# A four-layer graph network kernel on Trainium2: the last propagation as seven half-size products, with the sums of adj stored part by part

## The chip, the cores and the metric

The kernel runs on one core of one Trainium2 chip. The metric is device time in microseconds (us): how long the core takes for one execution, from its first instruction to the last result in DRAM. A core has five engines with instruction streams of their own: TensorE (PE; its weight loads are shown apart as PEld), VectorE (DVE), ScalarE (ACT), GpSimd (POOL) and SyncE (SP). In this kernel nearly all large loads and stores are issued by SP, one after the other. All data is float32.

## The reference, cut to what matters

The input x has 3327 nodes with 256 features; adj is a sparse, symmetric-pattern 3327 x 3327 matrix kept dense. Four layers follow one another, each as x = x + layer(relu(layernorm(x))). The first three multiply adj (with some change) by a 3327 x 256 matrix each. The change concerns layer 3, and the writes that layers 0 and 2 make for it:

```python
R = S + eye(N);  R = R / R.sum(-1)          # S is adj
Z = 0;  Xf = X;  Xa = X
for n in range(2):                          # the two steps
    A = top_p_attention(Xa)                 # softmax rows, only the entries that make up 0.9
    Xf = R @ Xf                             # propagation
    Xa = A @ Xa                             # attention
    Z = Z + Xf @ U1[n].T + Xa @ U2[n].T
return layernorm(X + Z) * ln_g + ln_b
```

## The kernel before

**Tiles and pairs.** The nodes are padded to T = 26 row tiles of 128 (P); D = 256 is the number of features, H = 13 half the number of tiles. Tiles p and p + 13 form a pair. `adj_t[m, :, k, :]` in DRAM is the block of adj that gives row tile m its share from column tile k. Matrix products keep a 128 x 128 block of adj as the weights and stream the right side through PE. The profile shows each float32 matmul of the program as two records.

**Half-size products.** In layers 0 to 2, a pair's product of a 2 x 2 matrix of blocks (rows p and p + 13, columns in two halves) with a right side cut likewise (two halves of rows, two halves of 128 features) is made of 7 products instead of 8, as in Winograd's form of Strassen's method. For that, sums of adj are needed (four for each pair: s1, s2, s4 and one that is written over a21, made on DVE in `Feed.add`, L489 to L492) and sums of the right side. A pair's columns are taken in three parts (`CUTS`) of five, four and four tiles; (p, c) is part c of pair p. `Feed` loads a part's four blocks of adj ahead (L473, SP), adds them, and, for the pairs in `keep`, also stores the four sums in `s_dram` (L495, SP). Layer 3 reads them from there. Layer 0 stores pairs 2, 4 to 12, layer 2 stores pair 0 and the odd ones (`KEPT`, L613), each with all three parts. In layer 2 DVE also counts the positive entries of each loaded block. The rows of a finished pair go through stages (`Pair`, L350 to L443); there PE turns h3a, the normalized rows (L373), which DVE makes at L400.

**Layer 3, step 1** (985 to 1745 us of the trace, with its last two phases between 1745 and 1876) already takes the propagation as 7 products for each pair: `FirstStepsPair` (L1095) loads a slab of 13 blocks (832 KB, SP) from `adj_t` or `s_dram` for each product n, POOL adds the identity to one block of the slab for n = 1, 4, 5 and 7 (L1110, for R = S + I), and PE issues 13 matmuls with 128 columns (L1140). A pair has two phases, products 1, 2, 5, 4 and then 7, 3, 6 (`PHASES`), each with an accumulator of one PSUM bank. After the first phase `half` (ACT, L1149) copies that bank, after the second `whole` (DVE, L1159 to L1163) adds the parts to the two rows. The slabs lie in a pool with three buffers, so that a load waits until PE has used up the third slab before it. `combine_h3` makes the right sides' sums `ts`, once.

**Layer 3, step 2** (1876 to 2606 us) takes the tiles one by one, m = 0 to 25. For each, PE does two things. `rows.finish(m)` is the attention: it turns the row of weights e in blocks (L181), ACT copies them (L184), PE multiplies them with `vs` (L192). Then `propagate_second` issues 26 matmuls with 256 columns (L1078) over two slabs (L1075), POOL having added the identity to one block (L1077). Between those matmuls other work is put at given points: the logits of the tile three ahead (`AHEAD` = 3; `prepare`, two groups of PE work at L923, exponentials on ACT at L944), and at point 20 the first turns of the next tile's attention (`rows.begin`). PE executes in the order in which the program is written (`manual_schedule`); the other engines' order is planned by the framework, which puts `high_priority` work ahead.

DVE searches the threshold of each row of weights (`search_steps`, L948): one pass over e at L993, four at L1002 with 26 MAX8 instructions between them (L1006), a chain of short ones, and the pass at L1022 which sets e to what is kept. PE turns e after that. The passes of ACT for the same search (L977, L982) are placed with `passes` and `passes_apart`.

`finish3` (L1225 to L1247) ends a tile: SP loads z (L1229) and x3 (L1231), POOL adds y, the attention's result (L1232), DVE adds the propagated rows (L1234) and takes mean and variance (L1236, L1238), POOL takes the root (L93, L95), DVE scales (L1241), POOL does three additions and multiplications (L1243 to L1245; DVE for the last tile), and SP writes the rows to `out` (L1247).

Of the kernel before, what the change touches and what calls it, by code (L numbers as in the profile page):

```python
# [11 lines left out]
F32 = mybir.dt.float32  # L12
# [10 lines left out]
D = 256  # L23
# [22 lines left out]
def kernel(  # L46
# [221 lines left out]
    def layers_0_to_2(again):  # L268
# [186 lines left out]
        class Feed:  # L455
# [24 lines left out]
            def add(self, p, c):  # L480
                a, b = CUTS[c]
                name = f"{tag}{self.layer}_{p}_{c}"
                q = self.quads.pop((p, c))
                s1, s2, s4 = (
                    raw.tile([P, 5, P], F32, tag=f"s{n}", name=f"s{n}_{name}", bufs=2)[:, : b - a, :]
                    for n in (1, 2, 4)
                )
                a11, a12, a22, a21 = (q[ij] for ij in QUADS)
                nc.vector.tensor_tensor(s1, a21, a22, ALU.add)  # L489
                nc.vector.tensor_tensor(a21, a11, a21, ALU.subtract)  # L490
                nc.vector.tensor_tensor(s2, s1, a11, ALU.subtract)
                nc.vector.tensor_tensor(s4, a12, s2, ALU.subtract)  # L492
                if p in self.keep:
                    for n, s in enumerate((s1, s2, a21, s4)):
                        nc.sync.dma_start(s_dram[:, p, n, a:b, :], s)  # L495
                self.ready[p, c] = a11, a12, s4, a22, s1, s2, a21
# [116 lines left out]
        KEPT = range(2, H, 2), [0, *range(1, H, 2)]  # L613
        IN_ORDER = [(p, c) for p in range(H) for c in range(len(CUTS))]

# [234 lines left out]
    def layer_3_in(tag, big, ep, w3, sm3, h3, kT0, ksum0, left, at_end):  # L850
# [3 lines left out]
        ts = new_nodes(f"ts3{tag}").rearrange("p t d -> p (t d)")[:, : 4 * H * P]  # L854
        ts = ts.rearrange("p (n k f) -> p n k f", n=4, k=H)
# [229 lines left out]
        def combine_h3(a, b):  # L1085
            def part(i, j):
                return h3[:, i * H + a : i * H + b, j * P : (j + 1) * P]

            t1, t2, t3, t4 = (ts[:, n, a:b, :] for n in range(4))
            nc.vector.tensor_tensor(t1, part(0, 1), part(0, 0), ALU.subtract)  # L1090
            nc.vector.tensor_tensor(t2, part(1, 1), t1, ALU.subtract)
            nc.vector.tensor_tensor(t4, part(1, 0), t2, ALU.subtract)
            nc.vector.tensor_tensor(t3, part(1, 1), part(0, 1), ALU.subtract)

        class FirstStepsPair:  # L1095


            def __init__(self, p):
                self.p, self.accs, self.slabs, self.name = p, {}, {}, f"{tag}_{p}"

            def load(self, n):
                p = self.p
                x = self.slabs[n] = slabs.tile([P, H, P], F32, tag="slab", name=f"slab3{tag}_0_{p}_{n}")
# [8 lines left out]
            def right(self, n, k):  # L1112
                if n in (1, 2, 3):
                    i, j = {1: (0, 0), 2: (1, 0), 3: (1, 1)}[n]
                    return h3[:, i * H + k, j * P : (j + 1) * P]
                return ts[:, {5: 0, 6: 1, 7: 2, 4: 3}[n], k, :]

            def steps(self, phase):
# [11 lines left out]
                for at, (n, k) in enumerate(units):  # L1130
                    bank, c = PLACE3[n]
                    start = bank not in self.accs
                    if start:
                        self.accs[bank] = new_acc(f"f0_{self.name}_{bank}")
# [90 lines left out]
        def finish3(m, y, acc, name):  # L1225
# [4 lines left out]
            x3 = w3.tile([P, 4, P], F32, tag="xf", name=f"x3_{name}").rearrange("p n f -> p (n f)")[:, :D]  # L1230
            nc.sync.dma_start(x3, x3_dram[:, m, :])  # L1231
            nc.gpsimd.tensor_tensor(z, z, y, ALU.add)  # L1232
            with tc.high_priority():
                nc.vector.scalar_tensor_tensor(z, acc[:, :D], rinv[:, m : m + 1], z, ALU.mult, ALU.add)  # L1234
# [140 lines left out]

        with tc.manual_schedule(engines=PE_ALONE):
# [40 lines left out]
            def propagate_first(n, at):  # L1417

                p, phase = divmod(n, 2)
                pair = pairs.setdefault(p, FirstStepsPair(p))  # L1420
# [40 lines left out]
            with tc.issue_after(left.made.ins):  # L1461
                combine_h3(0, H - 1)
            combine_h3(H - 1, H)
# [75 lines left out]
            steps_of_second = prepare(1, 1, kT1)  # L1539
            spare.append(made[1][0])  # L1540
            pairs[H - 1] = FirstStepsPair(H - 1)
# [17 lines left out]

        only_exp_and_ln()  # L1560
        with tc.manual_schedule(engines=PE_ALONE):
# [6 lines left out]
            second = find(1, 1, st1)  # L1568
# [6 lines left out]
            propagate_first(T - 1, merged(spread(prepare(1, 2, kT1), 4, 10), plan))  # L1575
            run(second)
            finder = find(1, 2, st1)
# [14 lines left out]
            for m in range(T):  # L1592
                plan, later = passes_apart(1, finder) if m + AHEAD < T else (passes(finder), {})
                if m == 0:
                    p, q = props
                    plan = merged(plan, {2: [p.scale, q.scale], 4: [p.turn], 5: [p.sums, q.turn], 6: [q.sums]})
                acc = rows.finish(m, plan)
                if m == 0:
                    nc.sync.dma_start(gs, ln_g.partition_broadcast(P))
                    nc.sync.dma_start(bs, ln_b.partition_broadcast(P))  # L1600
                y = attention_of_second_step(m, acc, dens.pop(m), f"{m}")
                plan = spread(prepare(1, m + AHEAD, kT1)) if m + AHEAD < T else {}
                plan = merged(plan, {20: [lambda: rows.begin(m + 1)]}, later)
# [84 lines left out]
```

## Time and profile before

| | |
|---|---|
| median of 3 runs (lowest, highest) | 2623.57 us (2622.97, 2629.18) |
| time of the profiled execution | 2624.72 us |
| its span in the trace | 2622.9 us, 45628 instructions |
| mean granted clock of PE | 0.994 |
| PE, DVE, ACT, POOL busy | 97%, 78%, 41%, 13% |
| layers 0 to 2 | 0 to 985 us |
| layer 3, step 1 | 985 to 1876 us |
| layer 3, step 2, and the end | 1876 to 2623 us |

The profile comes from one execution. Its span is what the trace covers; its time is the device time of that same execution, and both stand beside the median of the runs that were only timed. The busy time of an engine is the sum of its instructions; those that run side by side on different engines are counted on each. A line like `L1078` is the line of the kernel from which an instruction comes. "Idle before" and the name after `<-` tell what ended an engine's wait, as far as semaphores show it. A granted clock of 1.00 is the full speed of PE.

### The profile page before, as it was taken

How to read it: one execution, taken by the hardware profiler on the slowest of the kernel's cores; microseconds unless marked ns; L12 is line 12 of the kernel's file. 1: busy time of each engine (PE TensorE's matmuls, PEld its weight loads, DVE VectorE, ACT ScalarE, POOL GpSimd, SP SyncE). 2: the span in 40 equal slices, each digit the busy share in tenths (PEclk: the TensorE clock that was granted, in tenths of full speed). 3: DMA queues.
4: the chain of work that ended last, by engine and by line, in shares of the span. 5: the costliest groups of instructions: out<-in, count | busy, mean ns of one | idle time of the engine just before them, and what ended most of it. 6: DMA issues, size and time to landing. Idle time of an engine off the chain costs nothing. (4 is left out here: it accounts for less than half of the span.)

```text
span 2622.9 us, 45628 instructions
## 1 busy us (share of the span) xinstructions
PE 2539.9 (97%) x16993; PEld 2238.4 (85%) x16993; DVE 2058.3 (78%) x5464; ACT 1076.4 (41%) x2042; POOL 330.5 (13%) x461
## 2 busy tenths in 40 slices
PE   6999999999999999999999999998999999999997
PEld 6999999999999997878787878887878887888786
DVE  6666688888777778787878788884888888888883
ACT  2110123343111115555656556544555555555541
POOL 2000010000000001000000000000122232223321
PEclk9999999999999999999999999999999999999998
DMA  6677665555778856323232323232521222122111
GB/s 211 193 244 230 210 212 165 178 173 166 255 257 267 274 186 207 105 65 106 72 109 77 105 66 105 83 117 76 169 71 65 75 81 71 65 81 77 68 66 52
DMA packets 176477, 357.66 MB, mean 136 GB/s; under 512 B 19043, under 2 KB 78048, under 8 KB 176224
## 3 DMA queue, kind: packets, MB, share of 16 engines
q1 hardware_dynamic: 147904, 333.64, 39.3%
q10 hardware_dynamic: 28320, 20.80, 2.5%
q8 instruction: 140, 2.29, 0.4%
q14 instruction: 113, 0.93, 0.1%
HBM read 284.77 MB, written 67.89 MB: 134 GB/s over the span
## 5 line engine op out<-in xcount | busy, mean ns | idle before, releaser
L184 ACT COPY eT_a<-pt_a 128x512 f32<-128x512 f32 (+1 forms) x364 | 195.8, 554 | 394.5 <-PE pt_a L181 394.3
L192 PE MATMUL a<-h3a,eT_a 128*128 128x256 f32 x1352 | 323.5, 381 | 0.2 <-ACT eT_a L184 0.2
L192 PE MATMUL a<-vs,eT_a 128*128 128x256 f32 x1352 | 320.2, 381 | 0.2 <-ACT eT_a L184 0.2
L1078 PE MATMUL f<-fsa,slab3a 128*128 128x256 f32 x1352 | 312.7, 382 | 0.0
L1078 PEld LDWEIGHTS f<-fsa,slab3a 128*128 128x128 f32 x1352 | 249.8, 189 | 52.7 <-issue 17.4
L1006 DVE MAX8 cand_a<-w 128x8 f32<-128x128 f32 x1352 | 288.6, 278 | 4.5
L192 PEld LDWEIGHTS a<-h3a,eT_a 128*128 128x128 f32 x1352 | 244.2, 189 | 36.9 <-issue 5.9
L192 PEld LDWEIGHTS a<-vs,eT_a 128*128 128x128 f32 x1352 | 246.3, 190 | 31.5 <-ACT eT_a L184 0.7
L527 PE MATMUL acc_a<-tsa,s_a 128*128 128x128 f32 (+1 forms) x2028 | 268.5, 275 | 1.7 <-DVE tsa L335 1.7
L527 PE MATMUL acc_a<-tsa,a_a 128*128 128x128 f32 x2028 | 252.0, 276 | 2.0 <-DVE tsa L338 2.0
L527 PE MATMUL acc_a<-rhs,a_a 128*128 128x128 f32 (+1 forms) x2028 | 250.7, 276 | 0.1
L527 PEld LDWEIGHTS acc_a<-tsa,s_a 128*128 128x128 f32 x2028 | 247.4, 192 | 2.4 <-DVE tsa L335 2.2
L527 PEld LDWEIGHTS acc_a<-tsa,a_a 128*128 128x128 f32 x2028 | 240.6, 193 | 3.6 <-DVE tsa L338 2.6
L527 PEld LDWEIGHTS acc_a<-rhs,a_a 128*128 128x128 f32 x2028 | 238.4, 192 | 2.2 <-ACT rhs L416 0.4
L1002 DVE SCALAR_TENSOR_TENSOR w<-e_a,t_a 128x896 f32<-128x896 f32 x208 | 225.1, 1082 | 4.3
L944 ACT ACTIVATE e_a<-pl_a 128x1024 f32<-128x1024 f32 x208 | 177.8, 859 | 122.8 <-PE pl_a L923 122.8
L181 PE MATMUL pt_a<-ident,e_a 128*128 128x128 f32 x1352 | 198.9, 273 | 6.6 <-DVE e_a L1022 6.4
L181 PEld LDWEIGHTS pt_a<-ident,e_a 128*128 128x128 f32 x1352 | 165.6, 141 | 38.6 <-DVE e_a L1022 7.0
L993 DVE SCALAR_TENSOR_TENSOR w<-e_a,t_a 128x3328 uint8<-128x3328 f32 x52 | 191.6, 3684 | 4.0 <-DVE t_a L990 0.9
L1022 DVE SCALAR_TENSOR_TENSOR e_a<-e_a,all_least 128x3328 f32<-128x3328 f32 x52 | 191.6, 3685 | 1.8
L376 ACT ACTIVATE xT_a<-pt_a 128x512 f32<-128x512 f32 x52 | 30.8, 593 | 361.3 <-PE pt_a L373 340.5
L1140 PEld LDWEIGHTS f_a<-ts3a,slab3a 128*128 128x128 f32 x1352 | 161.5, 192 | 20.3 <-issue 18.5
(225 smaller groups left out, 3864.1 us busy)
## 6 DMA issues: line engine op xcount, KB each, us to landing
a_a<-in_adj_t_dram SPq DMA_DIRECT2D x312, 256.0 KB, 3.9
slab3a<-in_adj_t_dram SPq DMA_DIRECT2D x91, 832.0 KB, 4.7
a_a<-in_adj_t_dram SPq DMA_DIRECT2D x156, 320.0 KB, 3.5
slab3a<-s_dram SPq DMA_DIRECT2D x52, 832.0 KB, 4.5
s_dram<-s_a SPq DMA_DIRECT2D x78, 256.0 KB, 3.1
s_dram<-s_a SPq DMA_DIRECT2D x39, 320.0 KB, 3.5
x_dram<-x_a ACTq DMA_DIRECT2D x39, 256.0 KB, 4.0
s_dram<-a_a SPq DMA_DIRECT2D x26, 256.0 KB, 4.7
```

Of the source, the lines that this page charges most:

```text
L181: nc.tensor.transpose(pt[:, j, :], e[:, k * P : (k + 1) * P], ident)
L184: last_turned.append(nc.scalar.copy(eT[:, : len(blocks), :], pt[:, : len(blocks), :]))
L192: nc.tensor.matmul(acc[:, :width], ready[g][:, j, :], rhs[:, k, :], start=(k == 0), stop=(k == T - 1))
L376: nc.scalar.activation(dst.rearrange("p f n -> p (f n)"), pt.rearrange("p f n -> p (f n)"), func)
L527: nc.tensor.matmul(self.acc[:, g, at : at + wide], quads[n][:, k - CUTS[c][0], :], t, start=(k == 0 and n in (1, 4)), stop=(k == H - 1 and ...
L944: last_exp.append(nc.scalar.activation(dst, src, AF.Exp, accum_out=parts[:, c : c + 1]))
L993: nc.vector.scalar_tensor_tensor(junk, e, t, e, ALU.is_lt, ALU.mult, accum_out=got)
L1002: nc.vector.scalar_tensor_tensor(w[:, : (b - a) * P], eg, t, eg, ALU.is_lt, ALU.mult, accum_out=below[:, g : g + 1])
L1006: nc.vector.max(cand[:, 8 * k : 8 * k + 8], w[:, (k - a) * P : (k - a + 1) * P])
L1022: nc.vector.scalar_tensor_tensor(e, e, least, e, ALU.is_ge, ALU.mult, accum_out=st["kept"][:, m : m + 1])
L1078: nc.tensor.matmul(acc[:, :D], slab[g][:, j, :], xf[:, k, :], start=(n == 0), stop=(n == T - 1))
L1140: nc.tensor.matmul(self.accs[bank][:, c * P : (c + 1) * P], a, self.right(n, k), start=start, stop=last.get(bank) == (n, k), skip_group_ch ...
```

## The change

1. *Step 2 of layer 3.* The pairs p = 1 to 12 are propagated as 7 half-size products, by the class of step 1, now with arguments and called `PropagatedPair`; tiles 0 and 13 stay as they were. The tiles of step 2 are taken in the order 0, 13, 1, 14, 2, 15 and so on (`ORDER`). The attention of tile p is followed by the first phase of its pair, that of tile p + 13 by the second phase, and then `finish3` runs for both. The points of the other work are scaled to the phase's number of matmuls (52 or 39 instead of 26).
2. *Sums of the right side.* `combine` makes them for step 2's right side `fs` in tile 13's attention, in three cuts, in a buffer of its own (`new_ts`).
3. *Sums of adj.* What is stored in `s_dram` is chosen by part instead of by pair: of the 39 parts (p, c), counted in order, layer 2 stores those of pairs 0 and 1 and the odd ones (22), layer 0 the even ones from pair 2 on (17).
4. *Buffers.* x3 takes a buffer of tag hT instead of xf, since `half` uses xf now. One column of `w` is set to 0 between the two sections.

```diff
@@ -490,7 +490,7 @@
                 nc.vector.tensor_tensor(a21, a11, a21, ALU.subtract)
                 nc.vector.tensor_tensor(s2, s1, a11, ALU.subtract)
                 nc.vector.tensor_tensor(s4, a12, s2, ALU.subtract)
-                if p in self.keep:
+                if (p, c) in self.keep:
                     for n, s in enumerate((s1, s2, a21, s4)):
                         nc.sync.dma_start(s_dram[:, p, n, a:b, :], s)
                 self.ready[p, c] = a11, a12, s4, a22, s1, s2, a21
...
@@ -610,8 +610,10 @@
         def from_rows(dram_rows):
             return lambda p, x2: nc.sync.dma_start(x2, pair_of(dram_rows, p))
-        KEPT = range(2, H, 2), [0, *range(1, H, 2)]
         IN_ORDER = [(p, c) for p in range(H) for c in range(len(CUTS))]
+        KEPT = [], []
+        for n, (p, c) in enumerate(IN_ORDER):
+            KEPT[p < 2 or n % 2].append((p, c))
         def counter(i):
...
@@ -851,8 +853,11 @@
-        ts = new_nodes(f"ts3{tag}").rearrange("p t d -> p (t d)")[:, : 4 * H * P]
-        ts = ts.rearrange("p (n k f) -> p n k f", n=4, k=H)
+        def new_ts(step):
+            t = new_nodes(f"ts{tag}_{step}").rearrange("p t d -> p (t d)")[:, : 4 * H * P]
+            return t.rearrange("p (n k f) -> p n k f", n=4, k=H)
+
+        ts = new_ts(0)
         vs = big.tile([P, T, D], F32, name="vs")
...
@@ -1082,9 +1087,9 @@
         FIRST_PHASES = (1, 2, 3), (5, 4, 7, 6)
         PLACE3 = {2: (0, 0), 1: (0, 1), 4: (0, 2), 5: (0, 3), 6: (1, 0), 7: (1, 1), 3: (1, 2)}
-        def combine_h3(a, b):
+        def combine(h, ts, a, b):
             def part(i, j):
-                return h3[:, i * H + a : i * H + b, j * P : (j + 1) * P]
+                return h[:, i * H + a : i * H + b, j * P : (j + 1) * P]
             t1, t2, t3, t4 = (ts[:, n, a:b, :] for n in range(4))
             nc.vector.tensor_tensor(t1, part(0, 1), part(0, 0), ALU.subtract)
...
@@ -1092,15 +1097,16 @@
             nc.vector.tensor_tensor(t4, part(1, 0), t2, ALU.subtract)
             nc.vector.tensor_tensor(t3, part(1, 1), part(0, 1), ALU.subtract)
-        class FirstStepsPair:
-
-
-            def __init__(self, p):
-                self.p, self.accs, self.slabs, self.name = p, {}, {}, f"{tag}_{p}"
+        class PropagatedPair:
+
+
+            def __init__(self, step, p, h, ts):
+                self.step, self.p, self.h, self.ts = step, p, h, ts
+                self.accs, self.slabs, self.name = {}, {}, f"{step}{tag}_{p}"
             def load(self, n):
                 p = self.p
-                x = self.slabs[n] = slabs.tile([P, H, P], F32, tag="slab", name=f"slab3{tag}_0_{p}_{n}")
+                x = self.slabs[n] = slabs.tile([P, H, P], F32, tag="slab", name=f"slab3{tag}_{self.step}_{p}_{n}")
                 if n in (1, 2, 4):
                     i, j = {1: (0, 0), 2: (0, 1), 4: (1, 1)}[n]
                     nc.sync.dma_start(x, adj_t[p + i * H, :, j * H : (j + 1) * H, :])
...
@@ -1112,8 +1118,8 @@
             def right(self, n, k):
                 if n in (1, 2, 3):
                     i, j = {1: (0, 0), 2: (1, 0), 3: (1, 1)}[n]
-                    return h3[:, i * H + k, j * P : (j + 1) * P]
-                return ts[:, {5: 0, 6: 1, 7: 2, 4: 3}[n], k, :]
+                    return self.h[:, i * H + k, j * P : (j + 1) * P]
+                return self.ts[:, {5: 0, 6: 1, 7: 2, 4: 3}[n], k, :]
             def steps(self, phase):
...
@@ -1222,16 +1228,16 @@
                 if not last:
                     nc.sync.dma_start(fs_dram[:, self.m, :], rows)
-        def finish3(m, y, acc, name):
+        def finish3(m, y, rows, name):
             z = w3.tile([P, D], F32, tag="z", name=f"z1_{name}")
             nc.sync.dma_start(z, z_dram[:, m, :])
-            x3 = w3.tile([P, 4, P], F32, tag="xf", name=f"x3_{name}").rearrange("p n f -> p (n f)")[:, :D]
+            x3 = w3.tile([P, NC, P], F32, tag="hT", name=f"x3_{name}").rearrange("p c n -> p (c n)")
             nc.sync.dma_start(x3, x3_dram[:, m, :])
             nc.gpsimd.tensor_tensor(z, z, y, ALU.add)
             with tc.high_priority():
-                nc.vector.scalar_tensor_tensor(z, acc[:, :D], rinv[:, m : m + 1], z, ALU.mult, ALU.add)
+                nc.vector.scalar_tensor_tensor(z, rows, rinv[:, m : m + 1], z, ALU.mult, ALU.add)
             st = sm3.tile([P, 6], F32, tag="st3", name=f"st3_{name}")
             nc.vector.bn_stats(st, z)
             mv3 = sm3.tile([P, 2], F32, tag="mv3", name=f"mv3_{name}")
...
@@ -1373,6 +1379,9 @@
         APART = (3, 7, 11, 15, 19)
+
+        ORDER = [p + i * H for p in range(H) for i in range(2)]
+
         with tc.manual_schedule(engines=PE_ALONE):
             st0, made, dens, props = new_state("0"), {}, {}, []
...
@@ -1536,9 +1545,9 @@
                 11: [centre_second], 19: [lambda: next(steps)], 24: [lambda: next(steps)],
             })
             first_e, first_parts = made[0][:2]
-            steps_of_second = prepare(1, 1, kT1)
-            spare.append(made[1][0])
-            pairs[H - 1] = FirstStepsPair(H - 1)
+            steps_of_second = prepare(1, ORDER[1], kT1)
+            spare.append(made[ORDER[1]][0])
+            pairs[H - 1] = PropagatedPair(0, H - 1, h3, ts)
             for n in PHASES[0][:2]:
                 pairs[H - 1].load(n)
...
@@ -1557,6 +1566,8 @@
         if_failed(0, flags0, st0, kT0, redo_first, lambda name: first_e, redo_second_steps_first)
+
+        nc.vector.memset(w[:, 0:1], 0.0)
         only_exp_and_ln()
         with tc.manual_schedule(engines=PE_ALONE):
             st1 = new_state("1")
...
@@ -1565,16 +1576,16 @@
             p = props.pop(0)
             propagate_first(T - 2, merged(spread(steps_of_second, 0, 6), {3: [lambda: p.scale(last_exp)], 8: [p.turn], 12: [p.sums]}))
             p = props.pop(0)
-            second = find(1, 1, st1)
+            second = find(1, ORDER[1], st1)
             def pass_of_second():
                 with tc.issue_after(last_exp[-1].ins):
                     next(second)
             plan = {0: [lambda: p.scale(last_exp)], 3: [p.turn], 8: [p.sums], 15: [lambda: next(second), pass_of_second], 19: [pass_of_second]}
-            propagate_first(T - 1, merged(spread(prepare(1, 2, kT1), 4, 10), plan))
+            propagate_first(T - 1, merged(spread(prepare(1, ORDER[2], kT1), 4, 10), plan))
             run(second)
-            finder = find(1, 2, st1)
+            finder = find(1, ORDER[2], st1)
             fs.append(new_nodes(f"fs{tag}")[:, :, :D])
             for k in range(0, T, H):
                 for a, b in ((k, k + 6), (k + 6, k + H - 1)):
...
@@ -1589,26 +1600,47 @@
             rows = Rows(1, vs)
             rows.begin(0)
             flags1 = []
-            for m in range(T):
-                plan, later = passes_apart(1, finder) if m + AHEAD < T else (passes(finder), {})
-                if m == 0:
+            ts = new_ts(1)
+            ys = {}
+            for i, m in enumerate(ORDER):
+                ahead = ORDER[i + AHEAD] if i + AHEAD < T else None
+                plan, later = passes_apart(1, finder) if ahead else (passes(finder), {})
+                if i == 0:
                     p, q = props
                     plan = merged(plan, {2: [p.scale, q.scale], 4: [p.turn], 5: [p.sums, q.turn], 6: [q.sums]})
+                if i == 1:
+                    cuts = dict(zip((0, 2, 4), CUTS))
+                    plan = merged(plan, {k: [functools.partial(combine, fs[0], ts, *c)] for k, c in cuts.items()})
                 acc = rows.finish(m, plan)
-                if m == 0:
+                if i == 0:
                     nc.sync.dma_start(gs, ln_g.partition_broadcast(P))
                     nc.sync.dma_start(bs, ln_b.partition_broadcast(P))
-                y = attention_of_second_step(m, acc, dens.pop(m), f"{m}")
-                plan = spread(prepare(1, m + AHEAD, kT1)) if m + AHEAD < T else {}
-                plan = merged(plan, {20: [lambda: rows.begin(m + 1)]}, later)
-                if m == T - 1:
+                ys[m] = attention_of_second_step(m, acc, dens.pop(m), f"{m}")
+                plan = spread(prepare(1, ahead, kT1)) if ahead else {}
+                if i + 1 < T:
+                    plan = merged(plan, {20: [lambda: rows.begin(ORDER[i + 1])]}, later)
+                else:
                     plan = {4: [lambda: flags1.extend(failed("1", st1))]}
-                finish3(m, y, propagate_second(m, plan), f"{m}")
-                finder = find(1, m + AHEAD, st1) if m + AHEAD < T else None
+                p, phase = m % H, m // H
+                if p == 0:
+
+                    finish3(m, ys.pop(m), propagate_second(m, plan)[:, :D], f"{m}")
+                else:
+                    if not phase:
+                        pair = PropagatedPair(1, p, fs[0], ts)
+                    units = H * len(PHASES[phase])
+                    run(pair.steps(phase), {k * units // T: v for k, v in plan.items()})
+                    if not phase:
+                        pair.half()
+                    else:
+                        both = pair.whole()
+                        for j, k in enumerate((p, m)):
+                            finish3(k, ys.pop(k), both[:, j, :], f"{k}")
+                finder = find(1, ahead, st1) if ahead else None
         def redo_second(m, e, den, name):
             y = attention_of_second_step(m, rows_times(e, vs, w3, f"a1_{name}"), den, name)
-            finish3(m, y, propagate_second(m, {}), name)
+            finish3(m, y, propagate_second(m, {})[:, :D], name)
         at_end()
         spare.append(ep.tile([P, NP], F32, tag="e", name=f"spare{tag}"))
```

More of the change, by code (lines that the diff above doesn't have):

```diff
@@ L1133, in steps @@
                     if start:
-                        self.accs[bank] = new_acc(f"f0_{self.name}_{bank}")
+                        self.accs[bank] = new_acc(f"f{self.name}_{bank}")
                     if n not in self.slabs:
@@ L1419, in propagate_first @@
                 p, phase = divmod(n, 2)
-                pair = pairs.setdefault(p, FirstStepsPair(p))
+                pair = pairs.setdefault(p, PropagatedPair(0, p, h3, ts))
                 units = H * len((PHASES if p else FIRST_PHASES)[phase])
@@ L1461, in layer_3_in @@
             with tc.issue_after(left.made.ins):
-                combine_h3(0, H - 1)
-            combine_h3(H - 1, H)
+                combine(h3, ts, 0, H - 1)
+            combine(h3, ts, H - 1, H)
             for i in range(EARLY):
```

## The prediction

> **What bounds the kernel now.** I read the share of busy time first, then the stretches by stage, then the waits of PE, and last the timeline of the stages that are touched.
>
> ```profile
> span 2622.9 us, 45628 instructions
> PE 2539.9 (97%) x16993; PEld 2238.4 (85%) x16993; DVE 2058.3 (78%) x5464; ACT 1076.4 (41%) x2042; POOL 330.5 (13%) x461
> ```
> ```profile
> 690.00:985.00 295.00, 283.68 (x2500) 281.42 (x2500) 218.55 (x500) 31.17 (x101) 15.94 (x32) 0.99 0.77 252
> 1876.00:2606.00 730.00, 729.99 (x3673) 595.15 (x3672) 604.70 (x1787) 367.04 (x640) 191.46 (x216) 1.00 0.21 72
> ```
> ```profile
> PE pt_a L373 <- DVE h3a L400: 9.6, 6, 2.1
> ```
>
> The columns of the middle fence are length, busy time of PE, PEld, DVE, ACT and POOL, granted clock, DMA share, GB/s. Step 2 of layer 3 (1876 to 2606) is 730 us with no PE gap, so a PE slot taken out there is time taken out, as long as nothing else comes late. DVE is at 83% of that stretch. Layer 2 (690 to 985) has 11 us of PE gaps; 9.6 of them are six waits for h3a, up to 2.1 us each.
>
> [...] z+y on POOL (L1232) takes 0.72 us alone and 3.65 in the median, ending 0.6 us after the DVE instruction that covers it. [...] Here the grant dips to 0.72 and 0.66 for 5 us after gaps of only 2.60 us (at 318) and 2.08 (at 690).
>
> **The change, part by part.**
>
> ```profile
> 2569.79 9.23 PE L1078 MATMUL f<-fsa,slab3a 128*128 128x256 f32 x42
> 2578.86 1.03 PE L181 MATMUL pt_a<-ident,e_a 128*128 128x128 f32 x8
> ```
> ```profile
> 1835.96 7.09 PE L1140 MATMUL f_a<-ts3a,slab3a 128*128 128x128 f32 x62
> 1842.88 0.38 PE L141 MATMUL pt_f<-ident,xf_a 128*128 128x128 f32 x2
> ```
>
> *a. The products.* A matmul is two records. 42 wide records take 9.07 us, 216 ns each; 62 narrow ones, which step 1 has already in the form that step 2 gets, take 6.92 us, 112 ns each. A pair now is 2 x 26 matmuls = 104 wide records, 22.46 us. It becomes 7 x 13 = 182 narrow ones, 20.31 us. Twelve of the thirteen pairs change (tiles 0 and 13 stay): 12 x 2.15 = **-25.8 us**, all on PE, which sets the stage. The first phase of a pair (52 matmuls) gets 0.4 us longer, the second (39) 2.5 us shorter.
>
> *b. The sums in DRAM.* The same 39 parts of four sums each, but layer 2 writes about half of each pair instead of all of every second. In the stretches of 5 us the DMA is at 0.9 to 1.0 in the stored pairs and at 0.2 to 0.6 toward the end of the others, and the h3a waits (1.95, 1.64, 1.58, 2.09 and 1.33 us) fall in the stored ones: there the counting on DVE waits for loads of adj, and h3a stands behind it. Spread, most should go. Bounds: none, or 9.6 plus layer 0's gap at 318 (2.6 us and 1.8 of slow clock after it), 14; or up to 3 lost, if the pairs that were free start to wait. I take **-8**.
>
> *c. DVE.* The sums of fs (`combine`) are 12 operations of 640 or 512 elements, 0.82 and 0.68 us by L489: 8.7 us once, in tile 13. A tile's search now ends 8.8 us before PE turns the result (2054.4 against 2063.2) and DVE idles 3.6 us per tile, so it is nearly covered: 0 to 5, I take **+1**. Each pair adds `whole`, 1.8 us. Two tiles end together, and the second one's L1247 waits for a POOL chain that is still at the first one's three additions (2.3 us) and then its own root (0.9): a wait of about 1.4 us. A pair has about 52.3 us of DVE work and becomes 55.5, against a PE time of 58.1 that becomes 55.9: just covered. `half` is 0.59 us of ACT, at 50% in this stage, and the one-column memset is nothing beside it.
>
> *d. The end.* Today 3.9 us pass from the last matmul to the last addition. Four operations of `whole` (1.5 us, L1160 to L1163) come in front, tile 12 runs interleaved with the last tile, and its three additions are on POOL: +3 to +7, **+4**.
>
> *e. Loads.* 84 + 4 slabs of 832 KB instead of 52: 30 MB more over 700 us, 43 GB/s on 72. Volume is no bound. Their places in the queues are. Three slabs fit; a pair's fourth (n=4) can be loaded only when its first is used up, 5.0 us into the phase, and PE wants it at 12.0 (two logits groups, 3.2 us, and 78 records). In the built order SP first issues the output of both tiles of the pair before, then z and x loads, and the second z waits for that output to land. POOL then has to add the identity to the slab.
>
> ```profile
> 2043.99 0.41 DVE L1241 TENSOR_SCALAR z<-z,mv,r 128x256 f32<-128x256 f32 x1 [0.76 <-POOL r L95]
> 2046.85 0.34 SPq L1247 DMA_DIRECT2D out_dram<-z  x1
> 2048.78 0.32 SPq L1229 DMA_DIRECT2D z<-z_dram  x1
> ```
> ```profile
> 1307.38 3.68 DVE L993 SCALAR_TENSOR_TENSOR w<-e_a,t_a 128x3328 uint8<-128x3328 f32 x1
> 1308.78 2.60 POOL L1110 TENSOR_TENSOR slab3a<-slab3a,ident 128x128 f32<-128x128 f32 x1 [25.91 <-DMA slab3a<-in_adj_t_dram]
> 1313.52 0.45 POOL L1110 TENSOR_TENSOR slab3a<-slab3a,ident 128x128 f32<-128x128 f32 x1 [2.07 <-PE u L1187]
> ```
>
> Measured from the start of the second tile's scaling (today L1241, 1.1 us into the phase by my count): output issued +2.9, z +4.7, slab +5.1, landed and added from +9.7 (4.6 us in step 1) to +9.9. The next long DVE pass (L993) starts at +9.85: 8.8 us for the rest of the search and 1.0 for its first small steps. As the second fence shows, an addition that meets this pass ends after it: 2.60 us instead of 0.45. If POOL is first, the slab is ready 11.4 us into the phase and PE doesn't wait. If DVE is first, it is ready at about 15 and PE stands 3 us, in each of the ten pairs 2 to 11 for which DVE still searches. Both ends: 0 and 10 x 3 = 30, or 10 x 4.8 with the slow clock of such gaps; I take **0**, since the landing can be the 4.3 us of the fastest load, but it is close to even.
>
> Sum: -25.8 - 8 + 1 + 4 + 0 = -28.8. The profiled execution has a span of 2622.9 and a time of 2624.72, 1.15 above the median 2623.57. From its own time that gives 2595.9, from the median 2594.8. I predict **2596**.
>
> **Rivals.** (1) [...] For it: the two starts are 0.2 us apart at most, and two small loads go ahead of the slab. Against: the step 1 loads land within 4.6 to 4.9 us. It decides from eight lost pairs on: 2596 + 8 x 4.4 is past 2631; with ten, 2626 to 2644, and 2637 in the middle. Slower. (2) *A mixture*, since the difference is of the size of the scatter: three to six lost pairs, 2608 to 2622. (3) *DVE becomes the bound*: the margin is 0.4 us a pair; two more waits of 1 us would cost 12 x 1.6 = 19 us, 2615. Against: the search has slack before PE wants it. (4) *The sums cost instead of saving*: if every pair of layers 0 and 2 now waits as the stored ones did, b is about 0 to +3, 2604 to 2607; for it, layer 2's mean DMA share is 0.77 already. That the products aren't replaced is excluded by the built order: 91 narrow matmuls stand for each pair from the second on.
>
> **How the numbers follow.** Likeliest case, with (4) in it: 2588 to 2608, chance 0.50, all faster. Mixture or (3): 0.24, of which 0.13 faster, 0.10 the same, 0.01 slower. Nearly all pairs lost: 0.26, of which 0.03 the same and 0.23 slower. A measurement of this kernel tells about 0.3% from no change, 8 us: faster is below 2616, slower above 2631. That makes 0.63, 0.13, 0.24. The range 2588 to 2640 holds the likeliest case and the mixture, and the lower two thirds of rival 1.
>
> **What would show it.** Right: L1078 down to 104 records, the pair line with 2184 more at 112 ns, no PE gap in step 2, h3a waits under 3 us in sum, the last matmul about 33 us earlier. Wrong: PE waiting for slab3a or POOL in phase one of the pairs, each time beside an addition of over 2 us and a dip of the clock; or PE waiting for e_a in step 2 (DVE bound); or DVE waiting for adj in every pair of layer 2, with h3a behind it.

## The result and the profile after

The changed kernel takes 2618.88 us (median of 11 runs, 2614.18 to 2623.47) against 2623.57 (11 runs, 2620.92 to 2629.18). Taken run against run the ratio is 0.9977, 95% interval 0.9968 to 0.9987: 6 us faster, where 28 were forecast and 2588 was the low end and 2640 the high end of the range. The interval lies wholly below 1, so there is a gain, though it is under the 0.3% that the prediction named as the least that a measurement tells. The profiled execution has a span of 2617.1 us, 5.8 less than before, so the two traces hold about the whole difference. That is in part luck: in four other traces with the same layers 0 to 2 (experiments 3 and 4) step 2 begins between 1871 and 1878 us.

The first lines of the page after, then the stretch of step 2 by engine (length; busy time of PE, PEld, DVE, ACT and POOL; granted clock; DMA share; GB/s):

```profile
span 2617.1 us, 47704 instructions
PE 2518.9 (96%) x17929; PEld 2258.4 (86%) x17929; DVE 2081.1 (80%) x5537; ACT 1084.2 (41%) x2054; POOL 329.3 (13%) x485
```
```profile
1876.00:2622.00 746.00, 709.97 (x4612) 614.77 (x4611) 629.94 (x1868) 374.51 (x652) 193.41 (x244) 0.98 0.34 112
```

PE's busy time fell by 21 us and the span by only 5.8: the rest of what the products gave back, 15 us, is idle time now. The waits of PE in step 2 after (total, times, longest) name three of them:

```profile
PE f1a L1146 <- DMA slab3a<-in_adj_t_dram: 6.4, 2, 5.9
PE pt_a L181 <- DVE e_a L1027: 2.3, 1, 2.3
PE f1a L1146 <- POOL parts_a L944: 1.1, 2, 0.9
```

(In the last line the wait is for the identity addition at L1116; the small memset at L944 comes right behind it on POOL and carries the signal.)

The timeline of PE splits it up. From the first propagation matmul of step 2 to the end of the last, it was 730.3 us (1876.37 to 2606.71) and is 719.1 (1876.71 to 2595.82). A tile runs from the first propagation matmul to the next tile's; before, each took 29.04 us.

| Part of the path | predicted | the two traces show |
|---|---|---|
| a. 12 pairs, where nothing waits: 58.08 to 29.42 + 26.52 = 55.94 us | -25.8 | -25.7 |
| b. layers 0 to 2 and step 1 (start of step 2) | -8 | +0.3 |
| c. sums of fs: tile 0 takes 33.20 instead of 29.04 | +1 | +4.2 |
| e. pairs 2 and 3, first phase 30.64 and 30.61 instead of 29.42 | 0 | +2.4 |
| e. pair 12, first phase 33.52; without logits it should be 25.7 | 0 | +7.8 |
| d. last matmul to last addition, 4.0 to 8.6 us | +4 | +4.6 |
| rest, after the last addition | | +0.5 |
| sum | -28.8 | -5.8 |

(25.7 is 29.42 less 3.74, which is what a tile without logits saved before: 29.04 to 25.30.) The lines behind c, and behind the wait of pair 12, from PE's timeline after:

```profile
1891.80 1.67 PE L181 MATMUL pt_a<-ident,e_a 128*128 128x128 f32 x8 [2.27 <-DVE e_a L1027]
1893.27 3.46 PE L1083 MATMUL f<-fsa,slab3a 128*128 128x256 f32 x10
...
2559.00 3.07 PE L1146 MATMUL f1a<-tsa,slab3a 128*128 128x128 f32 x26
2568.02 1.23 PE L1146 MATMUL f1a<-tsa,slab3a 128*128 128x128 f32 x4 [5.95 <-DMA slab3a<-in_adj_t_dram]
```

Both waits cost more than themselves: ten records of L1083 took 3.46 us after the first, 2.33 in the tile that follows, because the clock that was granted fell (0.72 from 1890 to 1895, 0.50 from 2565 to 2570). Row b compares one trace with one, and is known to a few us only; experiment 1 tests it with repeated runs.

### The profile page after: what moved, and what is told of

It reads as the page before. It is cut to its first block, busy times and chain, and to the rows that moved or that the text cites. A ratio compares the mean times of both kernels' runs of the same rounds, so it can differ in the third digit from the quotient of the medians.

```text
span 2617.1 us, 47704 instructions
## 1 busy us (share of the span) xinstructions
PE 2518.9 (96%) x17929; PEld 2258.4 (86%) x17929; DVE 2081.1 (80%) x5537; ACT 1084.2 (41%) x2054; POOL 329.3 (13%) x485
## 5 line engine op out<-in xcount | busy, mean ns | idle before, releaser
L1116 POOL TENSOR_TENSOR slab3a<-slab3a,ident 128x128 f32<-128x128 f32 x100 | 116.8, 1169 | 731.0 <-DMA slab3a<-in_adj_t_dram 406.4
L1027 DVE SCALAR_TENSOR_TENSOR e_a<-e_a,all_least 128x3328 f32<-128x3328 f32 x52 | 193.5, 3721 | 1.7
L1146 PEld LDWEIGHTS f0a<-tsa,slab3a 128*128 128x128 f32 x1352 | 161.5, 192 | 20.2 <-issue 18.5
L631 DVE SCALAR_TENSOR_TENSOR pos<-a_a,pos 128x512 bf16<-128x512 f32 (+1 forms) x130 | 93.0, 716 | 102.2 <-DMA a_a<-in_adj_t_dram 101.2
```

The costliest lines, as they stand in the source:

```text
L631: nc.vector.scalar_tensor_tensor(s, q[i, j], 0.0, s, ALU.is_gt, ALU.add)
L1027: nc.vector.scalar_tensor_tensor(e, e, least, e, ALU.is_ge, ALU.mult, accum_out=st["kept"][:, m : m + 1])
L1116: nc.gpsimd.tensor_tensor(x[:, p, :], x[:, p, :], ident, ALU.add)
L1146: nc.tensor.matmul(self.accs[bank][:, c * P : (c + 1) * P], a, self.right(n, k), start=start, stop=last.get(bank) == (n, k), skip_group_ch ...
```

## The experiments

All ratios are to the kernel before, run on the same chip, with 95% intervals. "Step 2" is the stretch from first to last propagation matmul in the run's own trace. "Layer 2" runs from the start of PE's last group of prj_a matmuls (L383), the end of layer 1, to the start of the last turn of h3a (L373).

| Run | ratio | step 2, us | end of layer 1, us | layer 2, us |
|---|---|---|---|---|
| before | 1 | 730.3 | 697.0 | 288.3 |
| the changed kernel | 0.9977 (0.9968 to 0.9987) | 719.1 | 693.0 | 293.9 |
| sums_by_pair | 0.9970 (0.9959 to 0.9980) | 718.6 | 698.9 | 289.8 |
| before_by_part | 1.0009 (0.9999 to 1.0019) | 730.3 | 697.7 | 295.3 |
| no_sums | 0.9884 (0.9867 to 0.9901) | 718.9 | 688.3 | 276.5 |
| sums_layer2 | 0.9989 (0.9981 to 0.9997) | 718.7 | 687.9 | 301.0 |
| sums_layer0 | 0.9995 (0.9987 to 1.0004) | 718.8 | 718.5 | 278.0 |
| combine_late | 0.9962 (0.9949 to 0.9976) | 716.4 | 690.9 | 293.9 |
| slab_first | 0.9942 (0.9929 to 0.9955) | 710.7 | 690.8 | 291.7 |
| both | 0.9939 (0.9925 to 0.9953) | 710.7 | 688.4 | 295.4 |
| combine_pool | 0.9939 (0.9925 to 0.9952) | 714.5 | 688.9 | 294.0 |
| count_late | 0.9960 (0.9947 to 0.9974) | 713.9 | 693.3 | 292.5 |
| stores_act | 0.9987 (0.9978 to 0.9995) | 713.2 | 691.7 | 299.8 |

Three runs have the same layers 0 to 2 as the changed kernel and differ only in step 2 (combine_late, slab_first, both), as does combine_pool. In these four and the changed kernel layer 2 lies between 291.7 and 295.4 us and layer 1 ends between 688.4 and 693.0. The run before_by_part stores the same parts, and its layer 1 ends at 697.7. So a single trace places layer 2 to about 4 us and the end of layer 1 to 5 to 9, and smaller differences there are not read.

**1. The sums of adj: was spreading them worth 8 us?** Two runs undo or do that edit alone.

```diff
 sums_by_pair, in the changed kernel:
-        KEPT = [], []
-        for n, (p, c) in enumerate(IN_ORDER):
-            KEPT[p < 2 or n % 2].append((p, c))
+        KEPT = [(p, c) for p, c in IN_ORDER if p in range(2, H, 2)], [(p, c) for p, c in IN_ORDER if p in [0, *range(1, H, 2)]]
 before_by_part, in the kernel before:
-        KEPT = range(2, H, 2), [0, *range(1, H, 2)]
+        KEPT = [], []
+        for n, (p, c) in enumerate(IN_ORDER):
+            KEPT[p < 2 or n % 2].append((p, c))
...
-                if p in self.keep:
+                if (p, c) in self.keep:
```

> The changed kernel, with the sums stored by whole pairs as before (same 39 parts). Theory A (step b of the prediction: spreading the stores takes the waits for h3a away and is worth 8 us): this one is 8 us slower than the changed kernel, about 2627 us. Theory B (spreading only moves the waits to other pairs; the traces show the h3a waits at 9.9 us in 8 places after, 8.9 in 5 before): within 3 us of the changed kernel, 2616 to 2622, with layer 2 shorter by up to 5 us and layer 0 longer by up to 3.

> The kernel before, with nothing changed but the sums stored by part. Theory A: 8 us faster than before, about 2616 us, h3a waits under 3 us. Theory B: within 3 us of before, 2620 to 2627, with the h3a waits at about 10 us in layer 2 and more places than before.

Theory B holds in both: neither run differs from the kernel that it was made from by more than the intervals. The wait of PE for h3a in layer 2 in before_by_part:

```profile
PE pt_a L373 <- DVE h3a L400: 10.9, 7, 2.5
```

This view ends at 987 us; with the last wait, 0.7 us at 993, it is 11.6 us in eight places. Before, it was 9.6 us in six. In the changed kernel it is 10.6 us in nine places, and in sums_by_pair 5.5 in four. So spreading the stores spread the waits and did not shorten them. Layer 2 as a whole is 4 to 7 us longer with single parts (289.8 to 293.9, 288.3 to 295.3), at the edge of what single traces tell.

**2. What do the stores cost at all?**

```diff
 no_sums:
-                if (p, c) in self.keep:
+                if False:
...
-                    nc.sync.dma_start(x, s_dram[:, p, {5: 0, 6: 1, 7: 2, 3: 3}[n]])
+                    nc.sync.dma_start(x, adj_t[p + H * (n % 2), :, H * (n // 6) : H * (n // 6) + H, :])
...
 sums_layer2:
+        KEPT = [], IN_ORDER
 sums_layer0:
+        KEPT = IN_ORDER, []
```

> The changed kernel without the stores of the sums; layer 3 loads blocks of adj of the same size in their place, so its values are wrong and its loads are not fewer. If the stores make the waits for h3a (A, and B too): layer 2 loses its h3a waits and the slow clock behind them, 10 to 14 us with layer 0, about 2606 us. If the waits come from DVE's own order and not from the stores (theory C): h3a waits stay near 10 us and the time at 2616 to 2620.

> The changed kernel, with all 39 parts of the sums stored in layer 2 and none in layer 0. If a store's price is that of its traffic in a layer that is close to its loading limit, the 17 parts cost more in layer 2 than they did in layer 0: layer 2 longer by about 15/22 us for each part, 12 us, layer 0 shorter by 3 to 7: 2622 to 2628. If only the stored parts themselves wait and are hidden otherwise: 2616 to 2620.

> The changed kernel, with all 39 parts stored in layer 0 and none in layer 2. Layer 2 then ends as in the run without stores, about 15 us shorter from its first h3a to its last. If layer 0 has room (its waits are 2 to 3 us with 17 parts stored): 2604 to 2610. If layer 0 is as full as layer 2: it gets 12 to 16 us longer, 2616 to 2622.

Without stores the run is 24 us faster than the changed kernel (0.9884 against 0.9977), twice what was expected, and of the h3a waits of layer 2 only the last is left:

```profile
PE pt_a L373 <- DVE h3a L400: 0.7, 1, 0.7
```

So the stores do make the waits. Of the 17 us by which layer 2 got shorter, 9.9 are h3a waits, 2.0 two waits for sums of the right side (tsa, L335 and L338), and 3.4 two stretches of 5 us behind h3a waits, in which the clock was granted at 0.66; the rest is not assigned. Their price in layer 2 grows with their number: layer 2 takes 276.5 and 278.0 us with none, 288 to 290 with 21 parts by pair, 292 to 295 with 22 single parts, 301.0 with all 39. Layer 0 is another matter: layer 1 ends at 688 us with none and at 688 to 698 with 17 parts, but at 718.5 with 39. Its first 17 cost at most 10 us, the next 22 20 to 30. Both extremes come out slower than the split, sums_layer2 by 3 us with overlapping intervals and sums_layer0 by 5, against my expectation of room in layer 0.

What is late can be seen in the DMA issues of layer 2 (722 to 960 us; count, size, median us from issue to landing), with stores (the changed kernel) and without (no_sums):

```profile
a_a<-in_adj_t_dram SPq DMA_DIRECT2D x81, 256.0 KB, 4.7
```
```profile
a_a<-in_adj_t_dram SPq DMA_DIRECT2D x80, 256.0 KB, 3.4
```

A load of adj takes 4.7 us beside the stores instead of 3.4. The share of time for which the DMA engines are busy in this stretch goes the same way: 0.61 without stores, 0.77 with 22 parts, 0.95 with 39 (sums_layer2). DVE counts its positives among the operations that finish the pair ahead, and waits there; h3a stands behind. The timeline of DVE after shows one case, which became the 2.37 us wait of PE at 949 us:

```profile
934.51 0.29 DVE L550 TENSOR_TENSOR u_a<-u_a,p_a 128x128 f32<-128x128 f32 x1
938.81 0.69 DVE L631 SCALAR_TENSOR_TENSOR pos<-a_a,pos 128x512 bf16<-128x512 f32 x1 [4.01 <-DMA a_a<-in_adj_t_dram]
939.41 0.42 DVE L551 TENSOR_TENSOR y_a<-u_a,acc_a 128x256 f32<-128x256 f32 x1
```

Two runs, on top of slab_first (experiment 4), ask whether the place of the operations is to blame.

```diff
 count_late, in Feed:
     def load(self, p, c):
...
-                if self.count:
-                    self.count(p, c, q)
     def add(self, p, c):
...
                 q = self.quads.pop((p, c))
+                if self.count:
+                    self.count(p, c, q)
 stores_act:
-                        nc.sync.dma_start(s_dram[:, p, n, a:b, :], s)
+                        nc.scalar.dma_start(s_dram[:, p, n, a:b, :], s)
```

> The version with the fourth slab first, and the counting of positives on DVE (layers 0 and 2) written beside the sums of the same part instead of beside its loads; in the built order the two counts of a pair's last part then stand behind the additions that finish the pair ahead instead of among them. Theory: in layer 2 the stores fill the DMA, the loads of the next pair land late, DVE stands in a count for up to 4 us, and h3a stands behind it. With the counts one step later the h3a waits (10 us in 7 to 9 places) fall to 2 to 6 us and layers 0 to 2 get 4 to 10 us shorter: about 2602. Rival: the sums (L489) then wait in the same place for the same loads: h3a waits stay at 8 to 12, 2607 to 2612.

> The version with the fourth slab first, and the sums stored from ACT's queue instead of SP's, so that no load of adj stands behind a store that waits for DVE. If the loads are late because of their place behind the stores in SP's queue: h3a waits under 3 us and most of the 15 us that layer 2 loses to the stores come back, 2595 to 2600. If they are late because the DMA engines are full (0.9 to 1.0 in the bursts): layer 2 stays within 3 us of what it was, 2606 to 2612; slower than 2612 if ACT itself stands in the stores and its copies come late.

With the counts later, the h3a waits did fall as expected, to 2.4 us, and nothing was won, since PE waits for the counts and the sums themselves instead:

```profile
PE pc L640 <- DVE pos L635: 3.7, 3, 1.5
PE pt_a L373 <- DVE h3a L400: 2.4, 7, 0.7
PE acc_a L526 <- DVE s_a L491: 2.4, 2, 2.1
PE pkq_a L245 <- DVE counts L641: 1.7, 6, 0.3
```

With the stores on ACT's queue, DVE waits for the loads as long as in slab_first, from which this run is made (54.3 us in layer 2 against 54.0; 40.0 without stores). SP's order is thus not what makes the loads late. That speaks for the busy DMA engines (0.77 of the time with 22 parts, as above), but no run here separates them from other limits of the memory. PE's waits for h3a did fall, to 0.7 us, which that expectation gave as the sign of the other case; but PE now stands in other waits first, so this doesn't decide. For ACT's copies now stand behind stores:

```profile
PE pkq_a L245 <- ACT xT_a L376: 12.0, 5, 4.6
```

The run is 12 us slower than slab_first.

**3. The sums of fs.**

```diff
 combine_late:
-                    plan = merged(plan, {k: [functools.partial(combine, fs[0], ts, *c)] for k, c in cuts.items()})
+                    def combine_late(c):
+                        with tc.issue_after(kept_at[1, m].ins) if c[0] else nullcontext():
+                            combine(fs[0], ts, *c)
+
+                    plan = merged(plan, {k: [functools.partial(combine_late, c)] for k, c in cuts.items()})
```

(`kept_at[1, m]` is the pass at L1027 for that tile.)

> The changed kernel, with the second and third cut of the sums of fs held back until DVE has finished tile 13's search (its last pass over e). Theory: these 8.7 us stand in front of that search, where only 3.7 us of slack were, and so make PE's wait of 2.3 us and the slow clock after it (4.2 us in all): the wait goes, 4 us faster than the changed kernel, about 2614.5. Rival: the slack is lost at tile 1 instead, a wait of 2 to 4 us appears there, and the time stays at 2617 to 2620.

PE's wait for e is gone from step 2, and tile 0 takes 29.04 us. But pair 1's first phase grew from 29.42 to 30.58: slack is lost there, as the rival had it, though less (1.2 us for 2 to 4) and by another wait, that for the identity addition on POOL:

```profile
PE f1a L1146 <- DMA slab3a<-in_adj_t_dram: 5.8, 1, 5.8
PE f1a L1146 <- POOL parts_a L944: 2.6, 3, 1.1
```

Step 2 is 2.7 us shorter in the trace. By the ratios the run is 4 us faster than the changed kernel, as the theory had it, but the intervals overlap. So the cause of the wait is shown, and what its removal gains in all is not.

**4. The fourth slab.** In the changed kernel SP issued it for pair 12 only after two outputs, two x loads and two z loads (SP's issues, start and length; the last line is the slab). PE had used up the slab whose buffer it needed at 2556.1, so these 7.2 us lie between:

```profile
2556.02 0.34 SPq L1253 DMA_DIRECT2D out_dram<-z  x1
2556.41 0.43 SPq L1237 DMA_DIRECT2D x<-x_dram  x1
2559.41 0.34 SPq L1253 DMA_DIRECT2D out_dram<-z  x1
2559.80 1.85 SPq L1237 DMA_DIRECT2D x<-x_dram  x1
2561.69 1.17 SPq L1235 DMA_DIRECT2D z<-z_dram  x2
2563.28 0.33 SPq L1112 DMA_DIRECT2D slab3a<-in_adj_t_dram  x1
```

```diff
 slab_first (load() keeps the issue of n=4 as self.fourth):
+                    if self.step and not phase and at in (0, H):
+                        for early in (ns[:3], ns[3:])[at // H]:
+                            self.load(early)
+                        if at:
+                            with tc.issue_after(self.fourth.ins):
+                                while outs:
+                                    outs.pop(0)()
...
-                nc.sync.dma_start(z, z_dram[:, m, :])
+            with tc.issue_after(behind.ins) if behind else nullcontext():
+                nc.sync.dma_start(z, z_dram[:, m, :])
+                nc.sync.dma_start(x3, x3_dram[:, m, :])
...
-            nc.sync.dma_start(out[m * P : m * P + n, :], z[:n, :])
+            outs.append(lambda: nc.sync.dma_start(out[m * P : m * P + n, :], z[:n, :]))
...
```

(The edit also writes the loads of a pair's first three slabs together, at the start of its first phase.)

> The changed kernel, with SP's order altered in step 2: the fourth slab of a pair (n=4) is issued before the outputs of the pair ahead and before the z and x loads. Theory: in the last pair, which has no logits to cover it, PE's wait of 5.95 us for that slab, and the slow clock after it, come from those small transfers ahead of it in SP's queue (7.3 us), and so do the 2.4 us that pairs 2 and 3 lose to an identity addition that meets the DVE pass: about 9.5 us faster than the changed kernel, 2609. Rival: the slab's own buffer is what is late (n=1 used up 2.9 us into the phase, landing 4.7 after): the wait shrinks to 1 to 2 us at most, if SP isn't the cause it stays at 5 to 6 and the time at 2618.

> The fourth slab ahead of the small transfers, and the second and third cut of the sums of fs held back, together. If the two causes are separate they add: 4.2 and 9.5 us, about 2605 us, with no wait of PE over 1 us in step 2 and every pair at 55.9 us. If freeing one makes another late (DVE at 55.5 us a pair has no room left): waits for e appear in later pairs, 2609 to 2613.

slab_first is 9 us faster than the changed kernel (0.9942 against 0.9977, intervals apart), the size that its theory gave. The parts agree less well. In the traces step 2 is 8.4 us shorter: 5.5 us of it in pair 12 (7 expected), 1.3 in pairs 2 and 3 (2.4 expected; pair 2 still takes 30.48 us), and 1.6 in tile 0, which the edit doesn't touch and where the clock happened not to fall. The slab wait is gone from PE's waits in step 2:

```profile
PE pt_a L181 <- DVE e_a L1027: 4.5, 2, 2.4
PE f1a L1155 <- POOL parts_a L944: 0.8, 1, 0.8
```

Not all of pair 12's time came back: its first phase takes 28.0 us, not 25.7, because the next thing behind the slab was the last search. One of the two waits for e, 2.1 us, lies there. "both" added nothing to it, the second of its expectations, though in another form than written: the waits for e went from tile 0, and pairs 1 and 2 met the DVE pass with their identity additions instead (30.53 and 30.52 us), while pair 12 took 29.52 us instead of 28.02.

```diff
 combine_pool, on slab_first:
-functools.partial(combine, fs[0], ts, *c)
+functools.partial(combine, fs[0], ts, *c, engine=nc.gpsimd if k else nc.vector)
```

> The version with the fourth slab first, and the second and third cut of the sums of fs on POOL instead of DVE. Theory: PE's wait at tile 0 (2.3 us and the slow clock, 33.2 instead of 29.0 us) is DVE time of the sums of fs beyond the slack; with 5.4 us of the 8.7 taken off DVE it goes, and doesn't come back at tile 1 or 14 as it did when the sums were only held back: 4 us faster than the version with the fourth slab first, step 2 at 707 instead of 710.7 us from its first propagation matmul to its last. Rival: POOL and DVE hold each other up (additions on both that meet take as long as one after the other), DVE's passes get longer by what POOL takes, and the wait stays at 1.5 to 2.5 us.

The rival holds: PE waits 2.2 us for e, and tile 0 takes 33.1 us (31.6 in slab_first's trace, after a wait of 2.4 us without a fall of the clock). DVE's last pass before PE's turn ended 15.0 us after the start of step 2 in the changed kernel, 15.1 in slab_first and 14.9 here, with 5.4 us of work less. POOL's additions took 1.1 to 1.9 us each, and where the two engines met DVE took longer: the same addition of 640 elements takes 0.81 us in the changed kernel and 1.79 here, where it ended 0.68 us after the POOL addition that it met (L1096, 1877.36 to 1879.26). That all 5.4 us went this way is not measured.

```profile
1877.42 0.81 DVE L1098 TENSOR_TENSOR tsa<-fsa 128x640 f32<-128x640 f32 x1
```
```profile
1878.15 1.79 DVE L1098 TENSOR_TENSOR tsa<-fsa 128x640 f32<-128x640 f32 x1
```

The versions that beat both kernels are slab_first, both and combine_pool, alike within their intervals; slab_first is the simplest.

## Why the prediction was wrong, step by step

Three terms of the sum failed: b, taken as -8, is about 0; e, taken as 0, is 10.2; and c, taken as 1, is 4.2.

**a. The products: right.** 2.14 us a pair against 2.15 worked out, and all twelve pairs, as far as nothing waits.

**b. The sums: wrong by 8 us.** The failed step is "Spread, most should go". The waits lay in the stored pairs and not in the others, and I took concentration for the cause. The runs show that the stores as such are the cause, and that spreading them over all pairs spreads the waits without shortening them (9.6 us in six places before, 10.6 in nine after). What stood to be won shows only without stores: 24 us, not 9.6, since layer 0, other waits and the slow clock after the waits belong to it. The bound "up to 3 lost" in my own text was the better half of the range, and rival 4 the right case.

**c. The sums of fs: the term was mis-sized, 4.2 for 1.** I set 8.7 us of DVE work against 8.8 us of slack, from a tile in the middle of the stage. Tile 13 is the first, and there the slack was smaller. In the kernel before, DVE's pass and PE's turn that waits for it:

```profile
1881.54 3.69 DVE L1022 SCALAR_TENSOR_TENSOR e_a<-e_a,all_least 128x3328 f32<-128x3328 f32 x1
```
```profile
1889.03 1.04 PE L181 MATMUL pt_a<-ident,e_a 128*128 128x128 f32 x8
```

The pass ends at 1885.23, and 1889.03 less that is 3.8 us. 8.7 less 3.8 would have been a wait of 4.9. The pass ended 6.2 us later than before, counted from the start of step 2 (15.0 for 8.9), and PE waited 2.3, with 1.9 of slow clock after it. It is 6.2 and not 8.7 because an addition between the short instructions of the search costs less than its record: a round of that chain takes 0.89 us alone and 1.82 with two additions of 0.68 in it. combine_late, in which this wait is gone, shows that the sums made it.

**d. The end: right,** 4.6 us for 4. **DVE's balance a pair** held too: from pair 1 to pair 11 PE never waits for e. The 55.5 us were worked out a little too high: in pairs 4 to 8 DVE is busy for 50.8 us of each pair, waits 2.1 for POOL's roots and 1.5 for ACT, which is slack, where the prediction left 0.4. Rival 3 did not happen.

**e. The race for the fourth slab: the mechanism was right, its price and its place were not.** In pair 3 DVE was first, in pair 4 POOL (first POOL's additions of both pairs, then DVE's passes):

```profile
2063.57 3.36 POOL L1116 TENSOR_TENSOR slab3a<-slab3a,ident 128x128 f32<-128x128 f32 x1 [1.26 <-DMA slab3a<-in_adj_t_dram]
...
2119.53 0.46 POOL L1116 TENSOR_TENSOR slab3a<-slab3a,ident 128x128 f32<-128x128 f32 x1 [0.39 <-DMA slab3a<-in_adj_t_dram]
```
```profile
2062.92 3.69 DVE L998 SCALAR_TENSOR_TENSOR w<-e_a,t_a 128x3328 uint8<-128x3328 f32 x1
...
2120.04 3.69 DVE L998 SCALAR_TENSOR_TENSOR w<-e_a,t_a 128x3328 uint8<-128x3328 f32 x1
```

The addition that lost ended 14.9 us into the phase, as forecast ("about 15"). In the trace the two hold each other up. Where DVE was first (pair 3), POOL's addition took 3.36 us instead of 0.46. Where POOL was first, in five of the six pairs the short instruction of DVE that met the addition (L995) took 0.33 to 0.50 us instead of 0.22, and the pass began 0.04 to 0.05 us after the addition's end. In the sixth, pair 7, L995 took 0.22 us, and the pass overlaps the addition by 0.3 us and took 3.77 us instead of 3.69. What the two engines contend for is not shown. Of the ten pairs DVE was first in 2, 3, 10 and 11. But PE lost 1.2 us each in pairs 2 and 3 (in pair 2, 0.5 of it for the slab's landing) and nothing in 10 and 11, where the prediction had 3 to 4.8 for each. Two things were left out of the working. The block with the identity is number p of the slab, so PE wants it 0.22 us later with each pair. And the next tile's first eight turns (1.0 us) lie behind the second of that slab's 13 matmuls. So rival 1 (nearly all of the ten pairs lost) could not have cost 30 us even if every pair had lost: with a block ready at 14.9 us and wanted at 12.3 + 1.0 + 0.22 p, the waits of pairs 2 to 7 come to an estimated 4 us in sum, and the later pairs have none.

Its place was wrong as well: I limited the step to the ten pairs for which DVE still searches. Pair 12 has no pass to meet, but it has no logits either, so that PE comes to the fourth slab 8.9 us into the phase instead of 12.3, and there SP's queue, which I had written down (outputs and z loads ahead of the slab), was alone enough for a wait of 5.95 us and 1.9 more after it. slab_first, where this wait is gone, shows that this order is the cause.

Taken together, of the 23 us that were missing 8.3 lie in b, 3.2 in c, 10.2 in e, and 1.1 in the end. The measured time lies where the prediction put a mixture of lost and won pairs (2608 to 2622), but that is chance: the lost pairs cost 2.4 us, and the rest came from elsewhere.

Two slips in the prediction change nothing in this: the fifth wait for h3a before is 1.68 us in the trace, not 1.33, and the middle of 2626 and 2644 is 2635, not 2637.

## What to carry to other kernels

Slack must be read at the place where the work is added: the first and the last tile of a pipelined stage have another one than the tiles between, because what covers the work (here logits on PE, and DVE's lead) isn't there yet or no more. A wait that always coincides with some traffic suggests that the traffic matters, not that its clustering does; a run without the traffic tells the price before a run that moves it. In a queue that issues in order, small transfers that have to wait hold up the large one behind them: here 7.2 us in SP's queue became a wait of 5.95 us on PE.

## What the runs showed of the hardware that was not expected

The granted clock falls after some waits of about 2 us and not after others of the same length: after 2.27 us at 1891 in the changed kernel (0.72 in the stretch of 5 us) and 2.16 us at 1890 in combine_pool (0.66), not after 2.36 us at 1886 in slab_first (1.00), though the same instructions surround all three. Tile 0 took 33.2, 33.1 and 31.6 us. The stretches in the changed kernel and in slab_first (the third number from the end is the granted clock):

```profile
1890.00:1895.00 5.00, 3.20 (x13) 2.82 (x14) 5.00 (x6) 1.17 (x2) 0.00 (x0) 0.72 0.01 3
```
```profile
1885.00:1890.00 5.00, 3.75 (x22) 3.41 (x23) 5.00 (x6) 1.07 (x2) 0.00 (x0) 1.00 0.01 3
```

What decides whether the clock falls after such a wait is not shown.
